# Turning attention contexts by VectorE blocks and DMA instead of TensorE transposes, with expert weights split into two buffers

## The chip, the cores and the metric

The kernel is one program on one core of a Trainium2 chip. A core has TensorE (PE, matrix multiply[...]), VectorE (DVE), ScalarE (ACT), GpSimd (POOL) and SyncE (SP). Each runs its own list of instructions in order and waits on semaphores for the others. SP computes nothing here; its list is the queue of all DMA transfers, also taken in order. The metric is the device time of one execution in microseconds. Before the change it is 2339.45 us, the median of three runs (2335.71, 2339.45 and 2345.44 us).

## The reference

The input is 32 sequences of 56 tokens with 128 features, and for each sequence a context of 1500 rows with 128 features, all in float32. Two decoder layers follow each other:

```python
x = LN(x + windowed_self_attention(x))            # 16 heads of 8, window 32
x = LN(x + cross_attention_0(x, ctx))             # one head of 128
x = LN(x + top2_of_8_experts_0(x))                # 128 -> 512 -> 128, gelu
x = LN(x + recurrent_mixer(x))                    # convolution, gated scan
x = LN(x + cross_attention_1(x, ctx))             # 16 heads of 64, 1500 keys
x = LN(x + shared_and_top2_of_8_experts_1(x))     # 128 -> 256 -> 128, silu
```

Cross-attention uses the same context as keys and as values, in both layers:

```python
q = x @ Wq.T + bq;  k = ctx @ Wk.T;  v = ctx @ Wv.T + bv
out = (softmax(q @ k.T / sqrt(128)) @ v) @ Wo.T + bo        # layer 0
```

The kernel folds the key and value projections into the query and output side, so that scores are products of transformed queries with the raw context, and values are weighted sums of the raw context rows.

## The kernel before

**Tiling.** Two sequences form a pair (112 tokens), so there are 16 pairs. A context of 1500 rows is held as 125 partitions by 12 chunks: row 12p + c stands in partition p, chunk c (`PK`, `CK`). Scores need the context with the features on partitions ("turned": 128 partitions by 1500 columns); values need it as it is loaded. `cxN0` and `cxN1` hold the plain contexts of a pair for layer 0, with a column of ones; `amN0` and `amN1` hold them again for layer 1, and `amT`, a single buffer, holds one turned context for layer 1.

**Threads.** The kernel is written as Python generators that are stepped by a planner: `front` (self-attention and cross-attention 0 of a pair), `back` (experts 0, mixer and queries of layer 1, mostly for two pairs), `attention` (layer 1's cross-attention, the main thread: two blocks of 512 and 384 query columns for each of 32 contexts) and `post` (experts 1). The planner advances a clock of estimated PE time; from `FRONT_US`, `BACK_US`, `POST_US` and `PAIR_US` it works out how much of each side thread has to be emitted beside the main thread, and a number that a thread yields (`HOP`, `NORM`) says how much PE time is to pass before its next piece. The framework then places semaphores and fixes the order on each engine and on SP; PE, DVE, ACT and SP each keep that order on the chip.

**Cross-attention 0** (`cross_attention_0`, L495 to L581). Each of the two contexts is turned on PE: `tr` at L164 transposes a chunk of 125 by 128 into a PSUM bank, four chunks fill a bank, and L516 copies the bank into the SBUF tile `big0` or `big1`, by ACT for two of three banks and by DVE for the third. At L518 SP stores the turned context to a DRAM tensor `memT` (one per context). Then PE multiplies it with the padded queries (`qpad`), the probabilities are computed in `big0`, transposed back on PE (L544 on) and multiplied with `cxN`. The next pair's contexts are loaded at L208 when this is done.

**Layer 1's attention** (`attention`, L991). For each chunk a matmul with lhsT = columns of `amT` and 512 or 384 query columns gives scores; they are copied to SBUF at L1010, reduced at L1013, and the exponentials at L1097 and L1100 become lhsT of the value matmuls. `load_attended_T` (L1066) loads the next context's `memT` into `amT` after the last score matmul that reads it.

**Expert weights.** In `experts_0` one pool tag with four buffers takes up and down weights in turn (L646, L648): both halves of the next expert are requested before this expert's hidden units are computed. In `experts_1` gate, up and down weights of one expert share a tile with two buffers, in three DMAs at L819. A request for a buffer that is still being read makes SP wait, and all later rows of SP with it.

**SP's queue.** All loads and stores stand in SP's one list: 594 DMAs, whose completion is counted by eight semaphores used in turn.

The first two pairs are opened together by a leader and a follower thread, before the main thread starts; the folded layer-1 matrices `m1` and `n1` are made there.

Of the kernel before, what the change touches and what calls it, by code (L numbers as in the profile page):

```python
# [15 lines left out]
TP = 2 * S  # L16
# [9 lines left out]
E = 8  # L26
# [37 lines left out]

FRONT_US, BACK_US, POST_US, PAIR_US = 18.5, 37.0, 31.0, 81.5
BANK_US = 1.3
# [5 lines left out]
def decoder_kernel(  # L72
# [114 lines left out]

    cxN = [const.tile([PK, CK, D + 1], F32, name=f"cxN{i}") for i in range(2)]
    amN = [const.tile([PK, CK, D + 1], F32, name=f"amN{i}") for i in range(2)]
    amT = const.tile([P, CK * PK], F32, name="amT")  # L190
    for t in (*cxN, *amN):
# [92 lines left out]
    def fold_heads(hw):  # L284
        for dst, a, b, sc in ((m1, 0, 1, DH1**-0.5), (n1, 2, 3, 1.0)):
            for q in range(2):

                for par in range(2):
                    ps = bank(p_v, "v")
                    r0 = par * DH1  # L290
                    for i in range(4):
                        mm(
                            ps[:, i * D : (i + 1) * D],
                            hw[r0 : r0 + DH1, a, 4 * q + i, :],
                            hw[r0 : r0 + DH1, b, 4 * q + i, :],
                        )
                    nc.vector.tensor_scalar_mul(
                        dst[:, 8 * q + par : 8 * q + 8 : 2, :],
                        ps.rearrange("p (h d) -> p h d", h=4), sc,
                    )  # L300
                    yield
# [94 lines left out]

    HOP, NORM = 2.5, 7.5

# [91 lines left out]
    def load_x0(pp):  # L490
        cxN = contexts_0()
        for i in range(2):
            load_context(cxN[i], 2 * pp + i)

    def cross_attention_0(x, pp):  # L495
        cxN, qpad = contexts_0(), here(qpad0, "qpad")
# [7 lines left out]
            qpad[:, :, :S],  # L504
            linear(sqw("xk0"), qp, TP).rearrange("p (b s) -> p b s", b=2),
            1.0 / math.sqrt(D),
        )
        w = CS * PK
        cxT = [big_tile(i) for i in range(2)]
        for i in range(2):  # L510
            for k in range(NS):
                ps = bank(p_f, "f")
                for c in range(CS):
                    tr(ps[:, c * PK : (c + 1) * PK], cxN[i][:, k * CS + c, :D])
                copy = nc.vector.tensor_copy if k == 1 else nc.scalar.copy
                copy(cxT[i][:, k * w : (k + 1) * w], ps[:, :w])  # L516
                yield 0
            nc.sync.dma_start(memT[2 * pp + i], cxT[i][:, : CK * PK])  # L518
        yield 0.4

# [23 lines left out]
        for k in range(NS):  # L544
            ps = bank(p_f, "f")
            for c in range(CS):
                lo = (k * CS + c) * PK
                tr(ps[:PK, c * P : (c + 1) * P], pr[:, lo : lo + PK])
            copy = nc.scalar.copy if k == 1 else nc.vector.tensor_copy
            copy(  # L550
                pt[:, k * CS : (k + 1) * CS, :],
                ps[:PK].rearrange("p (c q) -> p c q", c=CS),
            )
            yield 0
        yield 0.8
        po = bank(p_f, "f")
        for c in range(CK):
            for i in range(2):
                mm(
                    po[64 * i : 64 * i + 64, : D + 1], pt[:, c, 64 * i : 64 * i + 64],  # L560
                    cxN[i][:, c, :], start=(c == 0), stop=(c == CK - 1),
                )
# [77 lines left out]
    def experts_0(xs):  # L640
        nj, nt = len(xs), len(xs) * TP
        nu = U0 // D

        def weights(e):
            wu = wst.tile([P, U0], F32, tag="w0", name="wu0", bufs=4)
            nc.sync.dma_start(wu, wup0[:, e * U0 : (e + 1) * U0])  # L646
            wd = wst.tile([P, U0], F32, tag="w0", name="wd0", bufs=4)
            nc.sync.dma_start(wd, wdn0[:, e * U0 : (e + 1) * U0])  # L648
            return wu, wd

        ws = weights(0)
        xT = to_features(xs, "xb", T)
# [15 lines left out]
        for e in range(E + 1):  # L668
            last = (ws, hT)
            if e < E:  # L670
                if e > 0:
                    ws = nxt
                if e + 1 < E:
                    nxt = weights(e + 1)
                hT = hidden_tile()[:, :, :nt]
                for u in range(nu):
                    nc.scalar.activation(  # L677
                        hT[:, u, :], linear(ws[0][:, u * D : (u + 1) * D], xT, nt), AF.Gelu,
                        bias=vec[:, C_BUP + e * nu + u : C_BUP + e * nu + u + 1],
                    )  # L680
                    yield 0
            if e == 0:
# [7 lines left out]
                for j in range(nj):  # L690
                    acc.append(plus(linear(pair(wT, j), bdn, D, TP), xs[j], "acc"))
            else:
                for j in range(nj):
                    nc.vector.scalar_tensor_tensor(  # L694
                        acc[j], down(last[1], last[0][1], nu, j),
                        w[:, j, e - 1 : e], acc[j], ALU.mult, ALU.add,
                    )
                    yield 0
        return acc

# [109 lines left out]
    def experts_1(xs, kept=None):  # L810
        nu, nj = U1 // D, len(xs)
        n = nj * TP

        def weights(e):
            if kept is not None:
                return kept[e]
            t = wst.tile([P, 3 * U1], F32, tag="w1", name="w1", bufs=2)
            for i, w in enumerate((gate1, up1, down1)):
                nc.sync.dma_start(t[:, i * U1 : (i + 1) * U1], w[:, e * U1 : (e + 1) * U1])  # L819
            return t  # L820

# [22 lines left out]
        acc = []  # L844
        ws, hT, nxt = w_sh, None, None
        for e in range(E + 2):
            last = (ws, hT)
            if e <= E:
                if e > 0:
                    ws = nxt  # L850
                if e < E:
                    nxt = weights(e)
                hT = mid.tile([P, nu, T], F32, tag="h1", name="h1", bufs=2)[:, :, :n]
# [15 lines left out]
            if e == 1:  # L869
                for j in range(nj):  # L870
                    a = tok_tile("pacc")
                    nc.vector.scalar_tensor_tensor(
                        a, down(last[1], last[0][:, 2 * U1 :], nu, j), 0.5, xs[j],
                        ALU.mult, ALU.add,
# [3 lines left out]
            elif e > 1:  # L878
                for j in range(nj):
                    nc.vector.scalar_tensor_tensor(  # L880
                        acc[j], down(last[1], last[0][:, 2 * U1 :], nu, j),
                        w[:, j, e - 2 : e - 1], acc[j], ALU.mult, ALU.add,
                    )
                    yield Two(0)
        return [normalize(a, "pz") for a in acc]

# [104 lines left out]
    def attention():  # L991
# [4 lines left out]
        for i in range(len(blocks) + 2):  # L996
            cur = None
            if i < len(blocks):
# [8 lines left out]
                for c in range(CK):  # L1007
                    ps = bank(p_s, "s")
                    mm(ps[:PK, :n], amT[:, c * PK : (c + 1) * PK], qT)
                    nc.scalar.copy(s[:, c, :], ps[:PK, :n])  # L1010
# [55 lines left out]
    def load_attended_T(b):  # L1066
        nc.sync.dma_start(amT, memT[b])

# [101 lines left out]
    for lo, hi in ((4 * D, 8 * D), (8 * D, N_SQ)):  # L1170
        nc.sync.dma_start(sq[:, lo:hi], sq_w[:, lo:hi])
    leader, follower = Thread(opening(0)), Thread(opening(1), aside)
    leader.step()
# [167 lines left out]
```

## Time and profile before

| | us |
|---|---|
| median of three runs | 2339.45 |
| profiled execution, its own time | 2352.06 |
| span of the profiled execution | 2350.4 |
| TensorE busy, matmuls | 2227.4 |
| VectorE busy | 1438.4 |
| ScalarE busy | 1359.2 |
| GpSimd busy | 251.5 |

The profile describes one execution; its span runs from the first to the last instruction. The granted TensorE clock was 0.976 of full speed over the span, lower in the first 140 us (0.90). In a group of instructions one reads, in this order: source line, engine, operation, tile written and tiles read, shape, count; busy time in us and mean duration of one in ns; the engine's idle time just before them and what ended it. `L164` and `L155` are the two helpers through which all transposes and matmuls go, so the tiles tell them apart. A float32 matmul appears as two matmul instructions with a weight load each; a transpose appears as one. `PEld` is the loading of the stationary operand, which overlaps with the running matmul. `SPq` is SP's queue. In a row of the table by stages stand the stretch, its length, busy time and count of PE, weight loads, DVE, ACT and POOL, then the granted clock, the DMA engines' busy share and GB/s.

The DMA engines are busy for 26.1% of the span. They moved 172.23 MB in 164304 packets.

### The profile page before, as it was taken

To read this page: it belongs to the slowest core of one execution; us is meant where nothing else is said; L and a number is where in the kernel's file an instruction comes from. 1 tells how busy PE (TensorE), PEld (TensorE's weight loads), DVE (VectorE), ACT (ScalarE), POOL (GpSimd) and SP (SyncE) were. 2 spreads that over 40 slices of the span, in tenths; PEclk is the share of its full clock that TensorE was granted. 3 is DMA by queue.
4 is the path that set the end of the run, shared out by engine and by line. 5 is a ranking of instruction groups with operands and counts; after the bars stand their busy time and mean duration, and the time that the engine had idled before them with its cause. 6 is when DMAs were issued, how large, how long until landed. Compare 5 with 4: busy or idle time off the path is not lost. (4 is left out here: it accounts for less than half of the span.)

```text
span 2350.4 us, 37566 instructions
## 1 busy us (share of the span) xinstructions
PE 2227.4 (95%) x14854; PEld 1753.8 (75%) x14854; DVE 1438.4 (61%) x2812; ACT 1359.2 (58%) x2344; POOL 251.5 (11%) x416
## 2 busy tenths in 40 slices
PE   7889999999999999989999899998999999999998
PEld 4667677677877788677786687776777788878777
DVE  4366654675666456655566565675656656676675
ACT  3456666557655664566645765556655576554462
POOL 3010110210111001110011100111001100010000
PEclk9799999999999999999999999999999999999999
DMA  7522122232322232211323023231232112111212
GB/s 194 149 83 71 63 59 93 41 87 74 108 72 56 72 84 71 75 46 67 91 71 92 22 72 97 74 82 34 69 87 82 42 54 74 52 38 27 83 47 77
DMA packets 164304, 172.23 MB, mean 73 GB/s; under 512 B 9464, under 2 KB 136864, under 8 KB 164000
## 3 DMA queue, kind: packets, MB, share of 16 engines
q1 hardware_dynamic: 164128, 169.82, 26.1%
q8 instruction: 118, 1.93, 0.4%
q14 instruction: 58, 0.48, 0.1%
HBM read 144.29 MB, written 25.49 MB: 72 GB/s over the span
## 5 line engine op out<-in xcount | busy, mean ns | idle before, releaser
L155 PE MATMUL v<-amN,s 125*128 125x129 f32 x5376 | 720.8, 279 | 12.8 <-ACT s L1100 12.8
L155 PEld LDWEIGHTS v<-amN,s 125*128 125x128 f32 x5376 | 681.1, 194 | 53.1 <-issue 30.3
L155 PE MATMUL s<-qo,amT 128*125 128x512 f32 (+1 forms) x1536 | 659.9, 550 | 1.6 <-ACT s L1010 0.9
L1010 ACT COPY s<-s 125x512 f32<-125x512 f32 (+1 forms) x768 | 397.5, 536 | 222.4 <-PE s L155 220.3
L1097 DVE TENSOR_TENSOR s<-s,nb 125x1536 f32<-125x1536 f32 (+1 forms) x256 | 397.6, 1564 | 45.3 <-ACT nb L1089 45.1
L155 PEld LDWEIGHTS s<-qo,amT 128*125 128x125 f32 x1536 | 266.1, 191 | 162.4 <-issue 93.9
L1100 ACT ACTIVATE s<-s 125x1536 f32<-125x1536 f32 (+1 forms) x256 | 338.4, 1326 | 78.5 <-DVE s L1097 70.8
L1013 DVE TENSOR_TENSOR m<-m,s 125x1024 f32<-125x1024 f32 (+1 forms) x256 | 280.7, 1096 | 90.5 <-ACT s L1010 85.7
L361 POOL TENSOR_SCALAR rs<-mv 112x1 f32<-112x1 f32 x126 | 47.9, 380 | 1199.7 <-DVE mv L355 1022.9
L1117 ACT ACTIVATE ao<-v,rz 128x128 f32<-128x128 f32 x224 | 80.8, 362 | 154.6 <-DVE rz L1115 153.6
L677 ACT ACTIVATE hT<-f,vec 128x224 f32<-128x224 f32 (+1 forms) x256 | 107.7, 437 | 86.7 <-PE f L155 84.7
L155 PE MATMUL f<-xb,wu 128*128 128x224 f32 (+1 forms) x512 | 142.4, 376 | 8.9 <-DMA wu<-in_wup_dram 4.2
L1013 DVE TENSOR_TENSOR m<-s 125x1024 f32<-125x1024 f32 x64 | 69.6, 1087 | 121.9 <-ACT s L1010 121.7
L155 PE MATMUL f<-wd,hT 128*112 128x128 f32 x960 | 131.0, 284 | 1.1 <-DVE acc L694 0.5
L155 PEld LDWEIGHTS f<-wd,hT 128*112 128x112 f32 x960 | 120.2, 185 | 13.4 <-ACT hT L677 2.1
L155 PE MATMUL f<-pxT,w 128*128 128x224 f32 (+1 forms) x512 | 107.0, 349 | 12.1 <-DMA w<-in_gate_dram 11.1
L155 PEld LDWEIGHTS f<-xb,wu 128*128 128x128 f32 x512 | 87.0, 203 | 38.7 <-issue 14.3
L155 PEld LDWEIGHTS f<-pxT,w 128*128 128x128 f32 x512 | 88.8, 190 | 22.5 <-issue 13.9
L1089 ACT COPY nb<-t 125x512 f32<-125x512 f32 x64 | 34.0, 531 | 102.0 <-PE t L164 99.6
L164 PEld LDWEIGHTS f<-ident,big 112*112 112x112 f32 (+1 forms) x420 | 51.5, 165 | 48.2 <-issue 20.6
L164 PE MATMUL f<-ident,big 112*112 112x112 f32 (+1 forms) x420 | 64.3, 284 | 23.1 <-ACT hT L677 6.7
L1115 DVE RECIPROCAL rz<-v 128x1 f32<-128x1 f32 x224 | 35.9, 160 | 78.1 <-PE v L155 77.6
(328 smaller groups left out, 2747.7 us busy)
## 6 DMA issues: line engine op xcount, KB each, us to landing
amT<-memT SPq DMA_DIRECT2D x32, 750.0 KB
amN<-in_mem_dram SPq DMA_DIRECT2D x34, 672.0 KB
memT<-big SPq DMA_DIRECT2D x30, 750.0 KB
cxN<-in_mem_dram SPq DMA_DIRECT2D x30, 672.0 KB
wu<-in_wup_dram SPq DMA_DIRECT2D x72, 256.0 KB
wd<-in_wdn_dram SPq DMA_DIRECT2D x72, 256.0 KB
w<-in_gate_dram SPq DMA_DIRECT2D x64, 128.0 KB
w<-in_up_dram SPq DMA_DIRECT2D x64, 128.0 KB
```

The source lines that it names most:

```text
L155: nc.tensor.matmul(ps, lhsT=lhsT, rhs=rhs, start=start, stop=stop)
L164: nc.tensor.transpose(ps, in_, ident[:k, :k])
L361: nc.gpsimd.tensor_scalar(rs, mv[:, 1:2], mul, add, ALU.mult, ALU.add)
L677: nc.scalar.activation(hT[:, u, :], linear(ws[0][:, u * D : (u + 1) * D], xT, nt), AF.Gelu, bias=vec[:, C_BUP + e * nu + u : C_BUP + e * n ...
L1010: nc.scalar.copy(s[:, c, :], ps[:PK, :n])
L1013: nc.vector.tensor_tensor(m, a, s[:, c - 1 : c + 1, :], ALU.max)
L1089: nc.scalar.copy(nb, ps[:PK, :n])
L1097: nc.vector.tensor_tensor(c, c, nb.unsqueeze(1).to_broadcast([PK, 3, n]), ALU.add)
L1100: nc.scalar.activation(c, c, AF.Exp)
L1115: nc.vector.reciprocal(rz, po[:, D : D + 1])
L1117: nc.scalar.activation(o, po[:, :D], AF.Copy, scale=rz)
```

## The change

- From pair 2 on (`pp > 1`) the contexts are no longer transposed on PE. `turned` calls a DVE transpose twice per context, once for even and once for odd chunks; each works on blocks of 32 by 32 elements within their own 32 partitions and leaves the blocks in `big0` or `big1`. Four DMAs per context, one for each 32 partitions, put the blocks in their places in `memT`, in runs of 64 elements (58 in the last); then one DMA loads `memT` back into `big0` or `big1` as the turned context.
- Two chunks lie interleaved in the turned layout: column (g, k, r) belongs to key k of chunk 2g + r. Score matmuls of layer 1 and the transposes of the probabilities therefore take every second column.
- Rows of `memT` are in another order of features for these contexts (row 4j + f holds feature 32f + j). The columns of `m1` and of a copy `xk0` of a weight are put in the same order. Pairs 0 and 1 are still turned on PE (`turned_at_once`), with the two-chunk column order; their rows are put in order when `amT` is loaded, by four DMAs.
- `cxN` gets 128 partitions; the last 32 are zeroed at the start.
- In both expert layers a weight tile holds one half (up, or gate and up; down), with two buffers for each. The half for the down product of the next expert is requested after this step's down products are emitted.
- `FRONT_US` becomes 15.0 instead of 18.5, and `turned` is followed by a yield of `TURN` = 10.

```diff
-    amT = const.tile([P, CK * PK], F32, name="amT")
+    amT = const.tile([P, CK // 2, PK, 2], F32, name="amT")
+    for t in cxN:
+        nc.vector.memset(t[P - 32 :], 0.0)
...
+    def turned(ts, b):
+        bigs = [big_tile(i) for i in range(len(ts))]
+        for i, (t, big) in enumerate(zip(ts, bigs)):
+            u = big[:, : CK * P].rearrange("p (f g i r) -> p r g f i", f=D // 32, g=CK // 2, r=2)
+            for r in range(2):
+                nc.vector.transpose(
+                    u[:, r], t[:, r::2, :D].rearrange("p g (f j) -> p g f j", j=32)
+                )
+            u = big[:, : CK * P].rearrange("p (h n) -> p h n", n=64)
+            rows_of = memT[b + i].rearrange("(j f) (g n) -> j (f g) n", f=D // 32, g=CK // 2)
+            for k in range(P // 32):
+                n = 2 * min(32, PK - 32 * k)
+                nc.sync.dma_start(
+                    rows_of[:, :, 64 * k : 64 * k + n], u[32 * k : 32 * k + 32, :, :n]
+                )
+        for i, big in enumerate(bigs):
+            nc.sync.dma_start(big[:, : PK * CK], memT[b + i])
+        return bigs
...
-        cxT = [big_tile(i) for i in range(2)]
-        for i in range(2):
-            for k in range(NS):
-                ps = bank(p_f, "f")
-                for c in range(CS):
-                    tr(ps[:, c * PK : (c + 1) * PK], cxN[i][:, k * CS + c, :D])
-                copy = nc.vector.tensor_copy if k == 1 else nc.scalar.copy
-                copy(cxT[i][:, k * w : (k + 1) * w], ps[:, :w])
-                yield 0
-            nc.sync.dma_start(memT[2 * pp + i], cxT[i][:, : CK * PK])
-        yield 0.4
+        if pp > 1:
+            cxT = turned(cxN, 2 * pp)
+            yield TURN
+        else:
+            cxT = []
+            for i in range(2):
+                cxT.append((yield from turned_at_once(cxN[i], 2 * pp + i, i)))
+            yield 0.4
...
-                lo = (k * CS + c) * PK
-                tr(ps[:PK, c * P : (c + 1) * P], pr[:, lo : lo + PK])
+                lo = (k * CS + c) // 2 * 2 * PK + c % 2
+                tr(ps[:PK, c * P : (c + 1) * P], pr[:, lo : lo + 2 * PK - 1 : 2])
...
-        def weights(e):
-            wu = wst.tile([P, U0], F32, tag="w0", name="wu0", bufs=4)
-            nc.sync.dma_start(wu, wup0[:, e * U0 : (e + 1) * U0])
-            wd = wst.tile([P, U0], F32, tag="w0", name="wd0", bufs=4)
-            nc.sync.dma_start(wd, wdn0[:, e * U0 : (e + 1) * U0])
-            return wu, wd
+        def weights(w, e, tag):
+            t = wst.tile([P, U0], F32, tag=tag, name=tag)
+            nc.sync.dma_start(t, w[:, e * U0 : (e + 1) * U0])
+            return t
...
+            if 0 < e + 1 < E:
+                downs[e + 1] = weights(wdn0, e + 1, "wd0")
...
-                    mm(ps[:PK, :n], amT[:, c * PK : (c + 1) * PK], qT)
+                    mm(ps[:PK, :n], amT[:, c // 2, :, c % 2], qT)
...
     def load_attended_T(b):
-        nc.sync.dma_start(amT, memT[b])
+        t = amT.rearrange("p g k r -> p (g k r)")
+        if b > 3:
+            nc.sync.dma_start(t, memT[b])
+            return
+        for f in range(D // 32):
+            nc.sync.dma_start(t[f :: D // 32], memT[b][32 * f : 32 * f + 32])
```

## The prediction

> **What bounds the kernel now.** I read the engine table first, then stages, then TensorE's waits, then the groups that the change touches.
>
> ```profile
> span 2350.4 us, 37566 instructions
> PE 2227.4 (95%) x14854; PEld 1753.8 (75%) x14854; DVE 1438.4 (61%) x2812; ACT 1359.2 (58%) x2344; POOL 251.5 (11%) x416
> ...
> q1 hardware_dynamic: 164128, 169.82, 26.1%
> ```
>
> TensorE (PE) is busy 95% of the span, no other engine more than 61%, and the DMA engines 26%. The table by stages says whether that holds everywhere:
>
> ```profile
> 0.00:140.00 140.00, 114.45 (x778) 86.05 (x779) 55.19 (x162) 55.95 (x131) 24.00 (x64) 0.90 0.62 166
> 140.00:600.00 460.00, 437.23 (x2972) 333.04 (x2973) 286.60 (x529) 284.53 (x494) 63.28 (x83) 0.97 0.25 69
> 600.00:1200.00 600.00, 575.54 (x3835) 455.71 (x3835) 370.44 (x713) 362.53 (x609) 65.30 (x104) 0.97 0.27 73
> 1200.00:1800.00 600.00, 571.99 (x3905) 451.98 (x3904) 370.05 (x721) 354.15 (x601) 64.75 (x107) 0.98 0.26 71
> ```
>
> After the first 140 us, PE (first figure behind the length) is idle 23, 24 and 28 us in 460, 600 and 600. So in these stages, where 14 of the 16 pairs pass through the cross-attention that is changed, the time is PE's work in PE's order; work taken from PE shortens the span, and a wait that PE runs into lengthens it by as much. PE's longest waits by releaser, the first two:
>
> ```profile
> PE v L155 <- ACT s L1100: 12.8, 7, 3.0
> PE f L155 <- DMA w<-in_gate_dram: 11.1, 10, 2.6
> ```
>
> The second is a late expert weight: SP, the in-order DMA queue, is held by earlier rows that wait for PE to free a buffer:
>
> ```profile
> SPq L819 <- PE f L155: 326.0, 51, 35.8
> SPq L648 <- PE f L155: 320.0, 50, 15.9
> ```
>
> **Part 1: transposes leave PE.** The groups:
>
> ```profile
> L164 PE MATMUL f<-ident,cxN 125*128 125x125 f32 x360 | 51.5, 276 | 0.7 <-DVE big L516 0.4
> L516 ACT COPY big<-f 128x500 f32<-128x500 f32 x60 | 34.7, 579 | 11.0 <-PE f L164 11.0
> L516 DVE COPY big<-f 128x500 f32<-128x500 f32 x30 | 20.3, 675 | 30.9 <-PE f L164 30.0 <-ACT big L516 0.8
> L1013 DVE TENSOR_TENSOR m<-m,s 125x768 f32<-125x768 f32 x128 | 122.2, 954 | 50.6 <-ACT s L1010 47.6
> ```
>
> A pair needs 2 contexts x 12 chunks = 24 transposes; pairs 2 to 15 lose them: 14 x 24 = 336 of PE's 14854 matmul instructions. The mean of 276 ns is a latency, since they overlap. Two prices remain: the group's busy time, 51.5 / 360 = 143 ns, and the spacing in PE's timeline:
>
> ```profile
> 1235.99 0.62 PE L164 MATMUL f<-ident,cxN 125*128 125x125 f32 x4
> 1236.45 1.02 PE L155 MATMUL s<-qo,amT 128*125 128x512 f32 x2
> ```
>
> Four hold PE from 1235.99 to 1236.45, 0.46 us, that is 115 ns each. The first gives 336 x 0.143 = 48 us, the second 84 x 0.46 = 39 us. The second is nearer to what the next instruction gains; I take 40 us.
>
> Copies out of PSUM go too: per pair four on ACT and two on DVE, 14 x 4 x 0.579 = 32 us off ACT and 14 x 2 x 0.675 = 19 us off DVE. Neither engine sets the pace: counted as nothing. In their place DVE gets 14 x 4 = 56 block transposes of 768 elements per partition. No such operation is in the trace; the nearest row is the 768-element fp32 operation at L1013, 954 ns: 56 x 0.954 = 53 us, net +34 us on DVE (61% to 63%). Twice that price would make it 65%, still far from the bound. What it costs is that PE's few waits on DVE get a little longer: +2 us (bounds 0 and 10).
>
> **Part 2: the detour through DRAM.** Each turned context is stored by four DMAs of 768 runs of 256 bytes (before: one of 128 rows of 6000 bytes) and read back by one of 128 rows: per pair 8 stores and 2 reads instead of 2 stores. PE's first score matmul now waits for the read-back; SP waits, before the read-back, for the stores to land, and all that stands behind it on SP (weights, the next keys in amT, the next contexts) waits with it. PE's order in the kernel as built gives the cover. I added up PE's work between the last of PE's releases that SP needs before the stores are all issued and the first score matmul, with PE's spacings: for pairs 2 to 15 it is 41, 41, 33, 37, 24, 40, 27, 31, 35, 33, 35, 33, 35 and 33 us. In pair 6 (24 us) three stores are still to come behind that release, in most others the second context's four.
>
> The need: four stores are 3072 packets on 16 engines, 192 each. By the trace's packet records a 512-byte packet took 27 ns in the stores of the output and 33 ns in the loads of the contexts, one of 6000 bytes 232 ns. The row for the shortest runs, 27 ns, gives 192 x 0.027 = 5.2 us. Against it stands a rule that speaks against this change: the Trainium skill, "DMA: Bandwidth & Descriptors", Specifications, says that below 512 bytes the engine does a read-modify-write, and doesn't state its price; no 256-byte run is in this trace. If it doubles the packet, 192 x 0.054 = 10.4 us. Around that: a store of memT landed 3.2 us after its issue, of which its 8 packets per engine took 1.9, so 1.3 us fixed; issuing four takes some 2 us (0.33 us for 128 runs, 0.62 for 1344); the two read-backs land 4.2 us (an amT load of the same size) + 1.9 us later. Together 5.2 + 1.3 + 2 + 6.1 = 15 us by the row and 20 us by the rule. Both lie under 24 us, the thinnest cover: stall 0 by either; I take 0 and keep the rule's packet for the likely case. In pair 4 all eight stores come behind the last release: 384 x 0.054 + 9.4 = 30 us of 33. If the cover were gone, each turn would cost its 15 to 20 us, 14 x 15 = 210 us at least.
>
> SP is held for those 15 to 20 us less the last landing, some 10 to 14 us. Next behind is amT, one buffer: loaded after a context's last score, needed after four tiles of values (4 x 24 half-matmuls x 0.11 us = 11 us and what is woven in). By PE's order its own release comes 12 us after the turn's last release in pairs 5 and 6 and 18 us or more after it elsewhere; so SP delays it in two pairs, by 2 us at most, and it lands in 4.2 of its 11 us. The DMA share grows by 86016 x 0.054 us / 16 / 2350 = 12% at most, from 26 to 38%.
>
> **Part 3: keys by two chunks.** The score matmuls now load weights with a step of 8 bytes (lhsT is every second element of amT), as do the transposes of the probabilities. All weight loads of the trace are dense:
>
> ```profile
> L155 PEld LDWEIGHTS s<-qo,amT 128*125 128x125 f32 x1536 | 266.1, 191 | 162.4 <-issue 93.9 <-ACT s L1010 20.3 <-ACT big L516 1.0
> ```
>
> They hide behind the running matmul, whose successors start 429 ns apart at 512 columns and 323 ns at 384. The price of the step is unknown: 0, or a load twice as long, 382 ns, which shows only at 384 columns, 768 x (382 - 323) = 45 us, and up to 168 x 0.19 = 32 us at the probabilities. The Trainium skill, "SBUF — State Buffer", in its note on cachelines, has lines of 16 bytes and no loss while two accesses hit a line; a step of 8 bytes is within that. No row measures it. I take 0 and keep 45 to 77 us for a rival.
>
> **Part 4: weights in halves.** Same bytes, same number of DMAs, but a load of down weights is no longer asked for one expert before its buffer is free, so SP is held less. Of the 11.1 us of waits on the gate weights I take 8 off (bounds 0 and 11).
>
> **Part 5: small things.** At the start two DVE memsets, a permuted write of m1 on DVE, a copy on GpSimd, and amT in four DMAs for contexts 0 to 3. They stand beside loads in the opening, where DVE is 39% busy; the first score of the main loop is at 142 us, some 90 us after the first amT load. +1 us. The planner's FRONT_US only moves pieces along PE; a shuffle of the remaining 60 to 80 us of PE's idle time is worth +-12 us.
>
> **The sum.** 2350.4 - 40 - 8 + 2 + 0 + 0 + 1 = 2305 us. That execution was slow among its kind: 2352.1 us against a median of 2339.45 (2335.7 to 2345.4). The difference, -45 us (1.9%), goes to the median: 2295 us.
>
> **Rivals.** 1. Likeliest: the sum above, 2272 to 2320 us (40 becoming 48, shuffle of 12, bounds of the waits).
>
> 2. Strided weight loads cost time. For it: 768 half-matmuls with only 323 ns of cover. Against: loads of 191 ns leave 132 ns of it. At twice the load: 2295 + 45 = 2340, with the probabilities 2372 us.
>
> 3. The other side: packets of 256 bytes are much dearer, and the read-back is later than PE's cover. Stalls begin in most pairs where 192 p + 9.4 us exceeds 33 us, at p = 123 ns, over four times the 512-byte row. At 150 ns a stall of 5 us in each of 14 pairs and about as much at pair 4 and at what waits behind on SP, 90 to 110 us: 2295 + 100 = 2395 us. The decision point against the gain of 45 us is near 135 ns.
>
> 4. The edit works but the order along PE turns out worse (PE waiting on scores, PSUM banks or amT): a stretched shuffle of 30 to 45 us, 2325 to 2340 us.
>
> **How the numbers follow.** Chances: first 0.74, second 0.08, third 0.10, fourth 0.08. A measurement of this kernel can tell about 0.5% (12 us) from no change: faster is below 2328, slower above 2351. Faster: the first and a third of the fourth, 0.76. Same: the rest of the fourth and half of the second, 0.10. Slower: 0.14. The range holds 8 in 10 from 2268 to 2350: below it 0.03, above it the third case and the upper half of the second. The likeliest case's own is 2272 to 2320.
>
> **What would show it.** Right: PE with 336 matmuls fewer and about 2180 us busy; 56 DVE transposes near 0.95 us; no line of PE waiting on a DMA into big; weight loads of s still near 190 ns; the wait on in_gate nearly gone. Wrong: PE's waits headed by big from memT or amT (third), weight loads of 300 ns or more and s starts further apart at 384 columns (second), or PE idle well above 123 us with no such DMA (fourth).

## The result, and the profile after

The changed kernel takes 2356.67 us (median of 4 runs, 2354.0 to 2357.62) against 2339.28 us before (4 runs, 2335.71 to 2345.44). The ratio of after to before is 1.007, 95% interval 1.0047 to 1.0093. The forecast was 2295 us, with 2268 to 2350 for 8 times in 10; the time lies above the range. The profiled execution took 2357.25 us and is typical of its kind.

The page of the changed kernel, first the lines that answer to the first fence of the prediction:

```profile
span 2355.5 us, 37226 instructions
...
PE 2230.1 (95%) x14518; PEld 1735.2 (74%) x14518; DVE 1468.3 (62%) x2842; ACT 1350.1 (57%) x2300; POOL 239.8 (10%) x417
...
q1 hardware_dynamic: 252128, 191.33, 35.1%
```

TensorE (PE) has 14518 matmul instructions, 336 fewer than before, and yet 2230.1 us of busy time where it had 2227.4. That is the whole riddle in one row: the work was taken away and the time stayed. The stages show where:

```profile
140.00:600.00 460.00, 428.69 (x2728) 315.67 (x2726) 292.43 (x523) 256.36 (x438) 50.43 (x76) 0.96 0.39 77
600.00:1200.00 600.00, 573.74 (x3731) 439.60 (x3732) 366.67 (x714) 358.94 (x605) 64.67 (x107) 0.96 0.39 88
```

In the first of these stages PE got through 2728 instructions, before it was 2972 in the same 460 us. The transposes of five pairs, 120, account for half of the 244; the other 124 are work not done by then, with 31 us idle instead of 23 and a clock of 0.96 instead of 0.97. From 600 to 1200 us it is 3731 against 3835, of which 96 were transposes: there PE keeps pace with the kernel before, but does not gain on it. Next, PE's waits by releaser (us in total, times, longest):

```profile
PE v L155 <- ACT s L1162: 16.2, 9, 5.2
PE f L155 <- ACT hT L722: 11.8, 14, 2.5
...
PE f L155 <- DVE oT L492: 3.8, 1, 3.8
```

The waits for the gate weights, 11.1 us before, are gone. There is no row of PE waiting for a DMA into the turned contexts or into amT. Summed over the whole table, the waits on DMA fell from 23.7 to 10.0 us, those on ACT grew from 41.8 to 57.6, and those on DVE stayed at 45. Last, the groups:

```profile
L511 DVE STREAM_TRANSPOSE big<-cxN 128x768 f32<-128x768 f32 x56 | 53.3, 962 | 12.0 <-PE f L164 6.8 <-ACT s L1162 4.6 <-issue 0.6
...
L164 PE MATMUL f<-ident,cxN 125*128 125x125 f32 x24 | 3.7, 279 | 0.1
...
L155 PE MATMUL f<-big,qpad 128*64 128x500 f32 x180 | 65.8, 615 | 0.0
...
L155 PEld LDWEIGHTS s<-qo,amT 128*125 128x125 f32 x1536 | 279.0, 197 | 174.3 <-issue 98.1 <-ACT s L1067 21.2 <-ACT big L461 1.6
```

The block transposes cost 962 ns each, as estimated (954). The transposes on PE are down to 24. The weight loads with a step of 8 bytes take 197 ns where dense ones took 191. One row is out of place: the scores of cross-attention 0, f<-big,qpad, whose instructions and shapes the change doesn't touch, had this row before:

```profile
L155 PE MATMUL f<-big,qpad 128*64 128x500 f32 x180 | 46.9, 604 | 0.2 <-ACT big L531 0.2
```

They take 18.9 us more. That is the first thing followed up.

### The profile page after: what moved, and what is told of

It reads as the page before. It is cut to its first block, busy times and chain, and to the rows that moved or that the text cites. A ratio compares the mean times of both kernels' runs of the same rounds, so it can differ in the third digit from the quotient of the medians.

```text
span 2355.5 us, 37226 instructions
## 1 busy us (share of the span) xinstructions
PE 2230.1 (95%) x14518; PEld 1735.2 (74%) x14518; DVE 1468.3 (62%) x2842; ACT 1350.1 (57%) x2300; POOL 239.8 (10%) x417
## 5 line engine op out<-in xcount | busy, mean ns | idle before, releaser
L155 PEld LDWEIGHTS v<-amN,s 125*128 125x128 f32 x5376 | 673.7, 194 | 74.4 <-issue 38.4
L155 PEld LDWEIGHTS s<-qo,amT 128*125 128x125 f32 x1536 | 279.0, 197 | 174.3 <-issue 98.1
L370 POOL TENSOR_SCALAR rs<-mv 112x1 f32<-112x1 f32 x126 | 37.3, 296 | 1232.3 <-DVE mv L364 1027.9
L155 PEld LDWEIGHTS f<-wd,hT 128*112 128x112 f32 x960 | 115.0, 180 | 18.5 <-issue 5.5
L740 DVE SCALAR_TENSOR_TENSOR acc<-f,wmix,acc 112x128 f32<-112x128 f32 x120 | 41.4, 345 | 89.2 <-PE f L155 89.0
```

The lines of the kernel that those rows point to most:

```text
L155: nc.tensor.matmul(ps, lhsT=lhsT, rhs=rhs, start=start, stop=stop)
L370: nc.gpsimd.tensor_scalar(rs, mv[:, 1:2], mul, add, ALU.mult, ALU.add)
L740: nc.vector.scalar_tensor_tensor(acc[j], down(last, wd, nu, j), w[:, j, e - 1 : e], acc[j], ALU.mult, ALU.add,)
```

## Experiments

All times are medians, and each set of runs had its own runs of the kernel before beside it, with medians from 2337.8 to 2344.7 us. So differences of under 5 us between sets are not read. Beside the medians I use a balance of PE's time made from each profiled execution: busy time counted at full clock ("work"), time lost to half clock while busy, and idle time. With 9 us at both ends they add up to the span. The last column is the longest stretch between two matmuls of layer 1's attention. From e4 on all runs but e18 have the paired scores of e1.

| run | median us | ratio to before (95%) | work | lost to half clock | idle | longest stretch without attention, 140 to 1000 us |
|---|---|---|---|---|---|---|
| before | 2338 to 2345 | 1 | 2176 | 52 | 114 | 7 |
| after | 2356.7 | 1.0047 to 1.0093 | 2170 | 60 | 117 | 62 |
| e1 paired scores | 2332.4 | 0.9944 to 0.9975 | 2139 | 60 | 124 | 37 |
| e2 before + halves | 2323.2 | 0.9895 to 0.9944 | 2173 | 38 | 101 | 7 |
| e3 after, whole weights | 2369.0 | 1.0092 to 1.0146 | 2172 | 65 | 117 | 65 |
| e4 e1 without turning | 2290.2 | 0.9762 to 0.9811 | 2141 | 31 | 107 | 28 |
| e5 e4 + transposes | 2290.6 | 0.9768 to 0.9803 | 2143 | 32 | 106 | 31 |
| e6 e1 - transposes | 2304.3 | 0.9826 to 0.9863 | 2143 | 42 | 110 | 41 |
| e7 e1, transposes spread | 2328.2 | 0.9929 to 0.9970 | 2152 | 46 | 120 | 62 |
| e8 e1, turned by PE | 2321.8 | 0.9894 to 0.9937 | 2174 | 37 | 102 | 7 |
| e9, e10, e11 pause 2, 20, 35 | 2328.2, 2322.0, 2366.9 | 0.994 to 0.9978, 0.9891 to 0.9943, 1.0086 to 1.0146 | 2144, 2146, 2155 | 50, 54, 63 | 130, 113, 142 | 36, 36, 67 |
| e12, e13 turned early | 2328.1, 2351.2 | 0.9915 to 0.9959, 1.0013 to 1.0049 | 2148, 2143 | 44, 62 | 126, 137 | 57, 36 |
| e14 e4 + long chain | 2324.3 | 0.9881 to 0.9946 | 2148 | 57 | 111 | 63 |
| e15 from pair 6 on | 2308.1 | 0.982 to 0.988 | 2148 | 39 | 110 | 20 |
| e16 from pair 4 on | 2301.1 | 0.9792 to 0.9846 | 2143 | 38 | 111 | 15 |
| e17 pairs 2 to 5 only | 2343.6 | 0.9983 to 1.0013 | 2164 | 50 | 120 | 37 |
| e18 e16, scores loose | 2324.3 | 0.9905 to 0.9939 | 2166 | 40 | 109 | 12 |

### The scores lost their neighbours

The two contexts of a pair use two halves of PE's columns (tile of 64 columns each). The changed kernel's timeline at pair 3 (start, length, engine, line, what):

```profile
324.89 1.89 PE L155 MATMUL f<-big,qpad 128*64 128x500 f32 x4
326.72 0.92 PE L155 MATMUL s<-qo,amT 128*125 128x384 f32 x2
327.56 1.89 PE L155 MATMUL f<-big,qpad 128*64 128x500 f32 x4
329.38 1.56 PE L155 MATMUL s<-qo,amT 128*125 128x384 f32 x4
330.88 1.06 PE L155 MATMUL f<-big,qpad 128*64 128x500 f32 x4
```

and that of the kernel before at the same pair:

```profile
283.81 1.90 PE L155 MATMUL f<-big,qpad 128*64 128x500 f32 x8
285.64 1.55 PE L155 MATMUL s<-qo,amT 128*125 128x384 f32 x4
287.12 1.06 PE L155 MATMUL f<-big,qpad 128*64 128x500 f32 x4
```

Each matmul leaves two records. Before, 8 records take 1.90 us, because those of the two contexts run at the same time. After, 4 records take 1.89 us: first two matmuls of one context, then attention work, then two of the other. Each runs alone at the price of a pair. Before, PE turned both contexts itself; after, each comes back with a read-back of its own. That the order is built apart because the two arrive apart is likely, but no run shows it. As built, 41 of the 90 such matmuls have no neighbour on the other half, before 1. **e1** adds an order, not a wait:

```diff
-            for i in range(2):
-                mm(ps[64 * i : 64 * i + 64, :w], qpad[:, i, :], cxT[i][...])
+            late = mm(ps[64:, :w], qpad[:, 1, :], cxT[1][...])
+            with tc.issue_after(late.ins):
+                mm(ps[:64, :w], qpad[:, 0, :], cxT[0][...])
```

> The changed kernel, with one ordering edge added: the score matmul of the second context is issued first and that of the first context directly behind it, so that the two 64-column halves of TensorE run side by side again (in the changed kernel 41 of these 90 matmuls stand alone, here none, in the kernel before 1). Theory A, lost side by side: the group's start-to-start time falls from 63.0 to about 45 us and the median from 2357 to about 2339 us (2333 to 2345). Rival B, clock and order: the group falls, but the time stays within 6 us of 2357, because TensorE spends the 18 us on other waits or at half clock.

Measured 2332.4 us, 24 us less than the changed kernel and 6 more than the group's 18. The group's row and the timeline of the paired kernel:

```profile
L155 PE MATMUL f<-big,qpad 128*64 128x500 f32 x180 | 43.2, 599 | 0.0
```

```profile
313.00 2.82 PE L155 MATMUL f<-big,qpad 128*64 128x500 f32 x12
```

All six matmuls of a pair in 2.82 us instead of 4.84 in three pieces. This group's busy time fell by 22.6 us. In the balance PE's work fell by 31 us, 19.5 of it in this group and 6.5 in the matmuls of the values (v), while idle time grew by 7. That the lone scores cost time is shown, and e18 below shows it once more; that they are all of the 24 us is not.

### What the turning itself costs

**e2** puts only the weights in halves into the kernel before; **e3** takes them out of the changed kernel; **e8** is e1 with PE turning every pair (no detour, layout by two chunks and halves kept, `FRONT_US` back at 18.5). Their edits are parts of the diffs shown above, so none is repeated.

> The kernel before, with only the expert weights in halves. The prediction's part 4: the 11.1 us of waits for in_gate go, 8 us are gained, 2331 us. Rival C, idle time only moves: the gate waits go and other waits of TensorE grow by as much, 2336 to 2343 us.

> The changed kernel with the expert weights loaded whole, as before. Theory A with the prediction's part 4: the 8 us of the weights are lost again, 2365 us. Rival C: within 6 us of the changed kernel, 2351 to 2363. Rival D, the halves are what made it slower: 2320 to 2340 us.

> The changed kernel with the later contexts turned by TensorE as the first two are (336 transposes back, copies on ScalarE and VectorE back, no store of 256-byte runs, front pace 18.5), keys by two chunks and weights in halves kept. If the layout by two chunks and the loads with a stride cost nothing: as the kernel before with halves only, 2323 us (2317 to 2330). If reading every second column is dear in the weight loads: 2335 us or more.

e2: 2323.2 us, 19 less than its runs of before: twice the 8 us of the prediction, and rival C falls. e3: 2369.0, 12 more than the changed kernel, so the halves help there too and rival D falls. e8: 2321.8 us, as e2: the layout by two chunks and the strided loads cost nothing that can be told. So the rest of the loss goes with the turning by VectorE and DMA, and 2322 us is what it has to beat.

**e4** leaves the turning out of the paired kernel: no transposes, no stores of runs; the read-backs and the later amT loads take as many contiguous bytes of the untransposed memory.

```diff
 def turned(ts, b):
...
-            for r in range(2):
-                nc.vector.transpose(u[:, r], ...)
...
-                nc.sync.dma_start(rows_of[:, :, 64 * k : 64 * k + n], ...)
...
-            nc.sync.dma_start(big[:, : PK * CK], memT[b + i])
+            nc.sync.dma_start(big[:, : PK * CK], flat_mem(b + i))
```

> The kernel with the paired scores, with the turning of the later contexts left out: VectorE's block transposes and the stores of their runs are gone, and the read-backs and the later loads for attention read as many contiguous bytes of the untransposed memory (so the values are not those of the reference). If the turning off TensorE costs nothing, as the prediction had it, within 5 us of the paired kernel. Rival E, the turning is dear in VectorE time or in DMA traffic: faster than the paired kernel by 10 us or more.

Measured 2290.2 us: rival E. The gain that the prediction summed up is there (31.6 us under e8, and 2290 us is within 5 of the forecast), but with the turning in, 42 us are lost again. In these two windows of e4, and then of e1, one sees where:

```profile
140.00:1000.00 860.00, 821.61 (x5559) 631.40 (x5558) 542.91 (x1026) 510.35 (x881) 108.14 (x165) 0.99 0.27 73
1000.00:2300.00 1300.00, 1237.68 (x8152) 996.20 (x8150) 817.12 (x1589) 775.38 (x1282) 111.27 (x182) 0.98 0.24 66
```

```profile
140.00:1000.00 860.00, 804.64 (x5294) 615.00 (x5293) 545.52 (x1015) 497.02 (x842) 98.09 (x159) 0.95 0.41 83
1000.00:2300.00 1300.00, 1258.06 (x8259) 1008.59 (x8259) 846.77 (x1595) 794.80 (x1314) 117.46 (x184) 0.99 0.31 74
```

Between 140 and 1000 us e1 has 17 us less PE busy time, and PE's clock falls from 0.99 to 0.95 (4% of 860 us is 34 us, part of it while PE was idle). After 1000 us e1 loses nothing more: counted at the matmuls of the values (v), it is 42 us behind e4 at the 2017th of 5376, which e4 starts at 1008 us, and 42 at the last. By the balance, PE's work is the same (2139 and 2141 us): e1 loses 17 us to idling and 28 us to half clock.

**e5** puts the transposes back into e4; **e6** has the stores and read-backs of e1, with the runs taken from the context as loaded and no transposes; **e7** cuts the four transposes of a pair into eight, with a `yield 1.5` after each.

> The kernel without the turning, with VectorE's 56 block transposes put back (their result is overwritten by the read-back of untransposed bytes, so the values are not those of the reference; the stores of 256-byte runs stay left out). Theory F, VectorE's time in one block: most of the 42 us between the kernel without the turning (2290) and the paired kernel (2332) comes back, 2320 to 2332 us. Theory G, the DMA detour: 2288 to 2298 us.

> The paired kernel with VectorE's block transposes left out: the stores of 256-byte runs are taken from the context as it was loaded, as many runs of the same length, and read back (so the values are not those of the reference). Theory F: 2288 to 2300 us. Theory G: 2320 to 2335 us, and the loads of weights and contexts land later than in the kernel without the turning.

> The paired kernel with the four block transposes of a pair of contexts cut into eight of half the size, and other work let in between them. Theory F: VectorE's waiting work gets through after 0.5 us instead of up to 3.9, and 10 to 25 us of the 42 are gained, 2307 to 2322 us. Theory G: no change, 2326 to 2338 us.

e5: 2290.6 us. VectorE's 54 us are free, and theory F falls; e7 (2328.2) agrees. e6: 2304.3 us, 14 of the 42 and outside the ranges of both theories. Nor are these 14 us a price that e1 pays: 8 of them are lost before the first matmul of the values, which starts at 166 us in e6 and at 157 in e4 and e1. With no transposes to wait for, SP issues pair 2's stores from 99 us on, among the expert weights of the opening; in e1 they come from 171 us on. So 28 to 36 us are left that neither part alone brings. What only both together have is the length of the chain: transposes, then stores, then read-backs, all between self-attention and the scores.

### Held banks, or late fronts

Theory H was that the scores claim both banks of the front's PSUM pool (tag f) in program order, so that nothing else of the front and back runs until the contexts are back. In e1 no such matmul runs for 201 us in all ahead of the score groups, in e4 for 46. **e9, e10 and e11** change the planner's pause ahead of the scores, `TURN = 10.0`, to 2, 20 and 35.

> The paired kernel with the pause between the turning and the scores, as the planner counts it, 2 us of TensorE work instead of 10. Theory H, the two banks of the front's PSUM pool go to the scores in program order, so that nothing else that uses this pool can run until the contexts have come back (in the paired kernel no such matmul runs for 201 us in all ahead of the 15 score groups, in the kernel without the turning for 46): more of it, 2338 to 2365 us. Rival G, it is the DMA traffic: 2326 to 2338 us, as with 10.

> The same with 20 us. Theory H: the stretches without such matmuls shrink to about 100 us in all, and of the 42 us over the kernel without the turning 15 to 25 are gained: 2305 to 2318 us. Rival G: 2326 to 2338 us.

> The same with 35 us. Theory H: the stretches are near those of the kernel without the turning, and what is left is the 14 us that the stores alone cost: 2295 to 2312 us; a front that ends too late for its place in the order would show as waits later on. Rival G: 2326 to 2338 us.

2328.2, 2322.0 and 2366.9 us. Only the middle one moves the way H says, by 10 us, and less than H asked; with 2 the time did not rise, and with 35 the stretches fell to 123 us and the time rose by 35. The last two lie outside the ranges of H and G alike. **e12 and e13** keep all the work but do transposes and stores ahead of the pair's self-attention, so that only the read-backs remain before the scores (pause 10 and 5). **e14** gives e4 a long chain with next to no work, eight round trips of 2 KB per context.

```diff
 def front(pp):
...
+        if pp > 1:
+            turn_out(cxN, 2 * pp)
         t = yield from self_attention(t)
```

> The paired kernel with the transposes and stores of the later contexts moved ahead of the pair's self-attention, so that only the read-backs lie between it and the scores; the same instructions and the same bytes. Theory H, the length of the chain: only the price of the stores (e6, 14 us over the kernel without the turning) is left, 2298 to 2310 us, and the stretches ahead of the scores without other matmuls of the front's PSUM pool fall from 201 us to under 70. Rival G, the work itself: 2322 to 2335 us, as the paired kernel.

> The same with the pause ahead of the scores 5 us instead of 10, since only the read-back is to be waited for. Theory H: within 6 us of the run with 10, 2295 to 2312 us. Rival G: 2322 to 2335 us.

> The kernel without the turning (2290 us; its values are not those of the reference) with a chain of eight round trips of 2 KB between memory and each context's tile ahead of the read-backs: a long chain with next to no work in it. Theory H: most of the 28 us comes back, 2310 to 2335 us, with stretches without the front's other matmuls as long as in the paired kernel (about 200 us in all). Rival G: 2288 to 2298 us.

e12: 2328.1 us, e13: 2351.2 us, although in e12 the stretches of H are down to 37 us: **theory H fell** as far as it is about held banks. These two runs pay for something else as well: pair 2's stores stand among the opening's expert weights, as in e6, and the first matmul of the values starts at 169 and 171 us, 12 and 14 later than in e4. Even without these 12 us e12 would lie above H's range, and e13 lies above that of G as well. e14 took 2324.3 us, 34 more than e4, with hardly any work added. That is within H's range, but the long chain explains it without held banks.

```profile
140.00:1000.00 860.00, 818.58 (x5403) 625.40 (x5401) 533.66 (x1015) 493.61 (x848) 100.16 (x161) 0.96 0.27 72
```

Its DMA share is that of e4, and yet PE's clock is down and 156 instructions are missing by 1000 us. A rival is that its 448 small transfers hold up the weights on SP, but PE waits for DMA for 13 us in all, in e4 for 11. So the length of the chain costs, between self-attention and the scores (e1, e14) and, by less, ahead of self-attention (e12). The last column of the table gave the next idea. In the changed kernel's timeline one sees PE without any attention work (s, v, t) for 62 us:

```profile
370.26 0.61 PE L155 MATMUL v<-amN,s 125*128 125x129 f32 x4
371.39 0.65 PE L155 MATMUL f<-xb,wu 128*128 128x224 f32 x2 [0.51 <-ACT hT L722]
...
397.74 3.75 PE L155 MATMUL f<-wd,hT 128*112 128x128 f32 x32
...
410.03 0.74 PE L155 MATMUL f<-sq,oT 128*112 128x128 f32 x2 [3.82 <-DVE oT L492]
410.56 0.58 PE L164 MATMUL f<-ident,h 112*128 112x112 f32 x2
413.33 3.87 PE L155 MATMUL f<-xb,sq 128*32 128x224 f32 x10 [2.19 <-DVE xb L768]
...
422.62 0.45 PE L164 MATMUL f<-ident,h 112*128 112x112 f32 x1 [2.42 <-DVE h L373]
424.31 0.45 PE L164 MATMUL f<-ident,h 112*128 112x112 f32 x1 [1.24 <-DVE h L373]
425.39 7.62 PE L155 MATMUL f<-xq,m 128*128 128x224 f32 x24 [0.63 <-ACT xq L347]
432.85 1.02 PE L155 MATMUL s<-qo,amT 128*125 128x512 f32 x2
```

Experts (wu, wd), the recurrent mixer (xb) and the query projections (xq) of pairs 2 and 3 run one after the other with nothing between them; when the first queries are out (425.39), attention goes on. Attention had caught up with the fronts. The length of such a stretch is no measure of the loss by itself (e4 has one of 28 us and takes 2290 us), but it points to the place. The scores of pair 3, on which these experts wait, begin at 324.9 us; before it was 283.8 us. The way to them, DVE and SP rows of the changed kernel:

```profile
264.41 0.98 DVE L511 STREAM_TRANSPOSE big<-cxN 128x768 f32<-128x768 f32 x1 [0.32 <-PE f L164]
```

```profile
267.41 1.30 SPq L518 DMA_DIRECT2D memT<-big  x2
274.08 0.60 SPq L518 DMA_DIRECT2D memT<-big  x1
284.93 2.41 SPq L1129 DMA_DIRECT2D amT<-memT  x4
287.39 5.10 SPq L518 DMA_DIRECT2D memT<-big  x5
292.60 1.27 SPq L522 DMA_DIRECT2D big<-memT  x1
```

60 us from the first transpose to the scores. The stores are held up once by what stands among them on SP; the second read-back lands at 303.9 us, and the order as built leaves another 21 us before it uses it. The lateness grows through the opening: pair 6's scores begin 110 us later than before (697 and 587 us); in e4, with the same front pace of 15.0, they begin 55 us later, so a front may be late by that much at no great cost. Theory I: only the fronts of the opening stage, due in quick succession (four within 2.1 of attention's pairs), can't afford that; later ones, one per pair of attention, can. **e15, e16** let PE turn the first pairs and VectorE the others; **e17** is the mirror, VectorE for pairs 2 to 5 alone.

```diff
+LAST = 3    # e16; 5 in e15
...
-        if pp > 1:
+        if pp > LAST:
             cxT = turned(cxN, 2 * pp)
...
-        if b > 3:
+        if b > 2 * LAST + 1:
             nc.sync.dma_start(t, memT[b])
...
-        along(front_line, FRONT_US, at)
+        nth = NPAIR - sum(not x[0].over for x in front_line)
+        along(front_line, FRONT_US if nth > LAST else 18.5, at)
```

> The paired kernel with only the pairs 6 to 15 turned by VectorE and DMA; pairs 2 to 5 are turned by TensorE like the first two, with the front pace of 18.5 for these. Theory I, late fronts in the opening stage: the early loss goes and the ten later pairs keep their gain of 2.4 us each over the kernel with TensorE turning (2322 us), less 0.5 to 1 for the stores: 2302 to 2314 us, and no stretch over 8 us without attention matmuls ahead of 1000 us. Theory J, the same price for every front: 2324 to 2332 us.

> The same with the pairs 4 to 15 turned by VectorE. Theory I: between the run from 6 on and the paired kernel, 2305 to 2322 us, later where a stretch without attention matmuls shows. Theory J: 2325 to 2333 us.

> The mirror: pairs 2 to 5 turned by VectorE, pairs 6 to 15 by TensorE. Theory I: the early loss stays and the later gain is gone, 2335 to 2352 us. Theory J: 2321 to 2327 us.

2308.1, 2301.1 and 2343.6 us. Theory J falls with each. e15 and e17 are where theory I had them, e16 is 4 us faster than its bound: pairs 4 and 5 can afford the detour as well. Turning pairs 2 and 3 by VectorE costs 31 us (e1 against e16), although e16 has 48 transposes more on PE, and turning the other twelve gains 21 us (e16 against e8). The front pace of 18.5 for these pairs goes with the edit; VectorE's turning at that pace was not run. The mirror (e17) loses its 22 us against e8 wholly ahead of 1000 us. One expectation was off: e15 has one stretch of 20 us without attention work, so the order still shifts. The same windows of e17 and then of e16:

```profile
140.00:1000.00 860.00, 810.12 (x5370) 623.61 (x5368) 535.82 (x1005) 502.87 (x861) 101.30 (x159) 0.95 0.35 77
1000.00:2300.00 1300.00, 1257.11 (x8318) 1005.25 (x8317) 827.96 (x1573) 776.36 (x1307) 113.65 (x182) 0.99 0.24 65
```

```profile
140.00:1000.00 860.00, 818.81 (x5525) 631.83 (x5524) 558.69 (x1042) 524.92 (x891) 110.35 (x163) 0.98 0.38 84
1000.00:2300.00 1300.00, 1247.63 (x8234) 1005.12 (x8233) 844.83 (x1624) 781.22 (x1291) 117.88 (x185) 0.99 0.31 73
```

The clock of 0.95 and the idle time of 50 us in the first window belong to the early turning, not to VectorE or DMA as such: e16 has more VectorE and DMA work there than e17, and yet a clock of 0.98 and 41 us idle.

**e18** is e16 with the scores as the changed kernel has them.

> The changed kernel with nothing but the pairs 2 and 3 turned by TensorE again; the scores are left to the order as the changed kernel has them (29 of 90 without a neighbour, where the run with the edge has none and the changed kernel 41). If the causes are separate: the run from pair 4 with the edge (2301 us) plus 0.45 us for each of the 29 lone matmuls, 13 us: 2310 to 2320 us. If the lone scores cost nothing once the fronts are in time: 2299 to 2305 us.

2324.3 us, 23 us over e16 and 4 over the expected range: the lone scores cost as much without late fronts as with them, so the two causes are separate. 14 us of it are in the score group's spacing (43.4 to 57.6 us, the 13 expected), 7.7 are more work in the matmuls of the values (v), as the changed kernel had 6.5 us more there than e1. Why those go with the order of the scores wasn't tried.

The version that beats both kernels is e16, 2301 us: ratio to before 0.9819 (0.9792 to 0.9846), with PE turning pairs 0 to 3, VectorE and DMA the others, the scores kept together and the weights in halves.

## Why the prediction was wrong

The gains were there. Three losses were not in the sum: the stores, the length of the chain, and the lone scores. From run to run: halves -19 (e2) and transposes off PE -32 (e8 to e4) lead to 2290 us; the turning put back adds 42 (e4 to e1) and the lone scores 24 (e1 to after). These are differences along one row of runs, so that they end at the measured 2356.7 proves nothing. That 2290 lies so near the forecast is partly luck: the transposes gave 8 us less than was counted, and the halves 11 us more.

- **Part 1, right.** 336 transposes for 40 us: their starts to the next instruction's shrank from 42.0 to 3.4 us, 38.6 us; as a gain of time 32 us. The 2 us for VectorE's share were 0 (e5), the block transpose 962 ns against 954.
- **Part 2, the failing step.** "Stall 0" came true in its own words: PE never waits for a read-back, each lands 8 to 27 us ahead of its scores. The error is what stood beside it: 24 to 41 us of PE work between the last release and the scores was read as cover that hides the detour. It is also delay for the front: the detour took 24 to 40 us from the first transpose to the last landing, and the scores began 44 to 60 us after the first transpose. For pairs 2 and 3, with 41 us of cover each, the front was what attention needed next. The step asked whether PE would wait at the scores, and not what is late behind the scores: experts, mixer and queries of the pair, and then attention. Price: 31 us for pairs 2 and 3 (e1 against e16) and 34 for a chain alone (e14), of the 42 in all. The packets were no part of it: 86016 packets of 256 bytes (232 in every fourth store) took 22 ns in the median and 36 in the mean, nearer to the row (27) than to the doubled price (54) that the rule might have meant. The stores' load on SP and DMA was counted as nothing, and e6 loses 14 us by it, 8 of them in the opening, where e1 does not; what the stores cost in e1 stays open.
- **Part 3, right.** 197 ns for a weight load against 191, and e8 equals e2.
- **Part 4, right in kind, too small.** 8 us were taken off, 19 measured (12 in e3 against after). The 11 us of waits went, and in e2 with them 14 us of half clock in the profiled execution, though that of the kernel before was itself some 10 us slow among its kind.
- **Part 5, the missing term.** "The planner's FRONT_US only moves pieces along PE", worth +-12 us. A look at PE's order, which was at hand and was used for the cover, would have shown 41 of 90 scores without their neighbour; at 0.45 us for each that is 18 us, and 24 were measured.
- **The rivals.** The second (strided loads) and the third (late read-backs) are refuted. The fourth, a worse order along PE, was the right kind at 0.08; it named scores and PSUM banks as what PE would wait for, and its end at 2340 us left out that two separate losses of order add up. Its sign, idle time well above 123 us, did not show: PE was idle for 125 us. The loss stood inside PE's busy time, as scores that ran alone and as matmuls at half clock.

## What to carry to other kernels

Work between an asynchronous step and its first reader is cover for the reader and delay for everything behind it: before calling a detour free, follow its result to the next place where the bound engine runs out of other work, and do so for the tightest stage, not the usual one. A new arrival by DMA also changes the order that is built, so list the neighbours of small matmuls that run side by side, before and after. Where a cost falls on the first few items alone, leave those as they were and change the rest.

## What the hardware showed that was not expected

A wait of PE can cost more than its length. Three windows around the 5.2 us wait that ends at 830.6 us in the changed kernel (the clock follows the five engines):

```profile
815.00:829.70 14.70, 10.14 (x50) 7.16 (x48) 13.38 (x35) 11.44 (x19) 0.93 (x1) 1.00 0.11 36
829.70:843.40 13.70, 12.79 (x26) 5.50 (x26) 8.25 (x15) 8.79 (x12) 3.93 (x4) 0.50 0.00 0
843.40:857.00 13.60, 13.55 (x96) 12.25 (x96) 5.02 (x10) 9.32 (x17) 0.40 (x1) 1.00 0.35 116
```

For 13.7 us from the end of the wait on PE is busy for 12.79, but at a clock of 0.50, and gets 26 instructions done where the next window does 96 (of other sizes). Half of the 12.79 us, 6.4, is lost on top of the 5.2.

The Trainium skill, "TensorE: Matmul & The Clock Gate", What's actually happening, has the clock halved after at least one idle window of some 3.4 us, in windows that run on freely. The lengths agree: apart from the last one of the execution, the half-clock stretches of the changed kernel are 3.4, 6.8, 10.2 and 13.7 us long, in the other runs up to 23.9, all multiples of 3.41. The condition does not: of the changed kernel's 19 such stretches only two follow 3.4 us without a matmul; in the 3.4 us ahead of the others PE was idle for 0.0 to 3.0 us. So here shorter waits went with half clock too; what sets it off is not shown. Over all, e1 against e4 idles for 17 us more and loses 28 us more at half clock. A sum of waits alone would have missed more than half of it.
